# Causal attention with a row mask on TensorE: one mask product a head, log subtraction first, and the key-major exp ahead of the last row exp

## Chip, cores and metric

The kernel runs on one core of a Trainium2 chip. The time is device microseconds (us) from the first to the last instruction of one execution, and what frames it; the median of several executions is compared. A profile is one execution, recorded instruction by instruction.

## The reference

The input x is 16 sequences of 512 tokens, 128 wide. It is layer-normalised, and goes into two branches that are added to x.

```python
xn  = layernorm(x)
q, k, v = xn @ Wq, xn @ Wk, xn @ Wv           # 16 heads, q and k 8 wide, v 64 wide
scores  = einsum('bhqd,bhkd->bhqk', q, k) / sqrt(8)
scores  = where(key > query, -inf, scores)     # causal
ctx = einsum('bhqk,bhkd->bhqd', softmax(scores), v)
xr, xk = mu * xn + (1 - mu) * shifted(xn)      # one mu each
ffn = sigmoid(xr @ W_r.T) * (relu(xk @ W_k.T)**2 @ W_v.T)
out = x + ctx @ Wo + ffn
```

## The kernel before

**Two passes over the scores.** The scores of a head are made twice. In the row-major pass (queries on partitions) the kernel makes masked scores, takes each row's maximum on VectorE (DVE), and lets ScalarE (ACT) take exp of them, in place in PSUM, only for the sum of each row. Ln of the sums and the maximum make one number a row, which is appended to q as two more rows of the contraction. In the key-major pass, ten units of work later, the scores come out of TensorE (PE) transposed and already normalised, and one exp gives the attention weights; GpSimd (POOL) zeroes the triangle above the diagonal, and PE weighs v with them.

**Units.** Work is cut into units, five to a group, where a group is two head pairs (four heads), and a batch (one sequence) has four groups, so 20 units a batch and 320 in all. The five kinds of a unit, 0 to 4, are rows of the tables `ROWS` (row-major blocks, lines 301 to 307) and `KEYS` (key-major blocks, lines 309 to 315). Each unit fills a PSUM tile `sm` of 128x1024 (row-major, two buffers) and a PSUM tile `sT` of 128x1024 (key-major, one buffer). Kinds 0 and 2 of the row pass have four row exps (two 384 wide, two 128 wide), kinds 1 and 3 have two (512 wide), kind 4 has four (256 wide). Every row exp is an ACTIVATE and a read of its accumulator.

**Order.** No scheduler moves anything: every engine's instructions run in the order in which `unit_work` (line 531) issues them, held there by the `_InOrder` wrappers (line 32, whose call is the L42 of most profile rows). In unit n the key-major pass works on unit n, the row exps on unit n + 10, and the row scores, mask and row maximum on unit n + 11. So a row exp in unit n uses the maximum from unit n - 1, and the row scores of unit n need the `sm` buffer that the row exps of unit n - 1 gave back.

In unit n PE does: `rowscores`, `scores`, `rowmask`, the listed pieces (in kind 1 after `weigh`), `weigh`, and in kind 0 `turn_stats`. DVE does: `take_ctx` (kinds 0 and 2), `rowmax`, the pieces, and in kind 0 `sub_logs` as the last piece and then `turn_stats`. ACT does: all row exps (`rowsum`), in kind 4 the Ln (`log_sums`), then the key-major exp (`weights`).

**Pieces.** The table `todo` (line 490) spreads the next sequences' projections over the units: `project_v`, `project_qk` (the q part in unit 10, the k part in unit 15 of a batch, each followed by two DVE conversions `qh, ql` or `kh, kl`), the feed-forward steps, `project_out` and so on. Pieces that need a PSUM tile take it from `m_tile` (line 150). From unit -1 on, all of them, the `pm` tile of `turn_stats` too, share one buffer; before that three are used in turn.

**The mask.** `rowmask` (line 341) adds a large negative number above the diagonal of each 128x128 diagonal block by a product of a 64-row bf16 identity (`id64`) with 64 rows of a bf16 mask (`mask64`). It takes two products a head, one for each half of the queries (`c`), the first 128 columns wide for each block and the second 64; with two heads that is four products a unit.

Of the kernel before, what the change touches and what calls it, by code (L numbers as in the profile page):

```python
# [9 lines left out]
FP = mybir.dt.float32  # L10
FR = mybir.dt.float32r
BF = mybir.dt.bfloat16
AF = mybir.ActivationFunctionType
ALU = mybir.AluOpType
# [3 lines left out]
P = 128  # L18
# [6 lines left out]
UNITS = 5  # L25
LEAD = 10
EPS = 1e-5
MASKED = -3.0e38
SIG_MIN = -87.5


# [16 lines left out]
def attn_ffn_kernel(  # L48
# [32 lines left out]
    const = ctx.enter_context(tc.tile_pool(name="const", bufs=1))  # L81
# [3 lines left out]
    one = ctx.enter_context(tc.tile_pool(name="one", bufs=1))  # L85
# [11 lines left out]
    pe, dve, act = _InOrder(tc, nc.tensor), _InOrder(tc, nc.vector), _InOrder(tc, nc.scalar)  # L97
    pool, sp = _InOrder(tc, nc.gpsimd), _InOrder(tc, nc.sync)
# [10 lines left out]
    for name, w in (("wq", Wq), ("wk", Wk)):  # L109
        t = one.tile([P, H * DK], FP, tag=f"{name}_n", name=f"{name}_n")  # L110
# [5 lines left out]
    for i, w in enumerate((W_r, W_k, W_v)):  # L116
        t = one.tile([P, D], FP, tag=f"ffn_n{i}", name=f"ffn_n{i}")
# [10 lines left out]
    ident = const.tile([P, P], FP, tag="ident", name="ident")  # L128
# [3 lines left out]
    fill = const.tile([3, 2, T], FP, tag="fill", name="fill")  # L132
# [157 lines left out]
    def ffn_out(b):  # L290
# [10 lines left out]
    ROWS = (  # L301
        ((0, 2, 0), (0, 0, 384)),
        ((0, 3, 0),),
        ((1, 2, 0), (1, 0, 384)),
        ((1, 3, 0),),
        ((0, 1, 0), (1, 1, 256)),
    )
# [11 lines left out]
    def unit_of(n):  # L319

        n, t = divmod(n, UNITS)
        b, g = divmod(n, NPAIR // 2)
        return (b, g, t) if 0 <= b < B else None


    stats, sms = {}, {}
# [14 lines left out]
    def rowmask(b, g, t):  # L341

        ends = [to + (i + 1) * P for _, i, to in ROWS[t]]
        step = ends[-1] - ends[0] or P
        for c in range(2):
            for u in range(2):
                s = slice(64 * u, 64 * u + 64)
                cols = sms[b, g, t][:, u, ends[0] - P :]
                if len(ends) > 1 and step > P:
                    cols = cols.rearrange("q (m k) -> q m k", k=P)[:, 0 :: step // P, 64 * c :]  # L350
                else:
                    cols = cols.rearrange("q (m k) -> q m k", k=P)[:, :, 64 * c :]
                pe.matmul(
                    cols, id64[s, c, :],
                    mask64[s, c : c + 1, 64 * c :].to_broadcast([64, len(ends), P - 64 * c]),
                    start=False, stop=(c == 1),
                )

    def rowmax(b, g, t):
        if t == 0:  # L360
# [14 lines left out]
                negm[:, :, w, i], sm[:, :, to : to + (i + 1) * P], AX.X, ALU.max, negate=True  # L375
            )

    def rowsum(b, g, t):
        negm, z = stats[b, g]
        sm = sms.pop((b, g, t))  # L380
        for w, i, to in ROWS[t]:
            for u in range(2):
                cols = sm[:, u, to : to + (i + 1) * P]
                act.activation(
                    cols, cols, AF.Exp,
                    bias=negm[:, u, w, i : i + 1], accum_out=z[:, u, w, i : i + 1],
                )

    def log_sums(b, g):
        lz = stat.tile([P, 2, 2, NB], FP, tag="lz", name=f"lz_{b}_{g}")  # L390
# [3 lines left out]
    def sub_logs(b, g):  # L394
        negm, z, lz = stats[b, g]
        dve.tensor_tensor(lz, negm, lz, ALU.subtract)
# [12 lines left out]
    def put_stats(b, g):  # L409

        for n, half in enumerate(stats.pop((b, g))):
            for u in range(2):
                r = 64 * u + RS + n
                pool.dma_start(
                    out=qs[b % 2].bitcast(FP)[r : r + 1, 2 * g : 2 * g + 2, :].rearrange(
                        "o p (i t) -> o (p i) t", t=P
                    ),
                    in_=half.bitcast(FP)[2 * NB * u : 2 * NB * u + 2 * NB],
                )
# [15 lines left out]
    def weights(b, g, t):  # L435
        e = ep.tile([P, 2, 512], FP, tag="e", name=f"e_{b}_{g}_{t}")
        act.activation(e, sts.pop((b, g, t)), AF.Exp)
        for w, j, to in KEYS[t]:

            diag = e[:, :, to : to + P]  # L440
            pool.affine_select(
                out=diag, in_=diag, compare_op=ALU.is_ge, fill=0.0, base=0,
                pattern=[[0, 2], [1, P]], channel_multiplier=-1,
            )
            es[b, 2 * g + w, j] = e[:, :, to : to + T - j * P]
# [41 lines left out]

    todo, turns, puts = {}, {}, {}  # L490

    def at(n, f, *args):
        todo.setdefault(n, []).append((f, args))
# [4 lines left out]
    for b in range(B):  # L498
        n0 = b * per
        if b + 1 < B:  # L500
            r = 0 if b else 7
            at(n0 + r, ffn_r, b + 1)
            at(n0 + r + 1, ffn_exp, b + 1)
            for c, n in enumerate((3, 8, 13, 18) if b else (11, 13, 14, 18)):
                at(n0 + n, ffn_sig, b + 1, c)
            for m, n in enumerate((1 if b else 3, 5, 12, 13, 14, 16, 17, 18)):
                at(n0 + n, project_v, b + 1, m // 2, m % 2)
            at(n0 + 7, mix_prev, b + 1, 1)
            at(n0 + 9, mix, b + 1, 1)
            at(n0 + 11, ffn_k, b + 1)  # L510
            at(n0 + 19, ffn_out, b + 1)
            for m, n in enumerate((-1, -1, 0, 0, 4, 4, 5, 5) if b else (0, 0, 0, 0, 4, 4, 5, 5)):
                at(n0 + n, spread_qk, b + 1, *SPREAD[m], slice(0, NPAIR // 2))
            for m, n in enumerate((8, 9, 9, 10, 10, 14, 14, 15)):
                at(n0 + n, spread_qk, b + 1, *SPREAD[m], slice(NPAIR // 2, NPAIR))
        if b + 2 < B:
            at(n0 + 4, deviation, b + 2)
            for c in range(NB):
                at(n0 + (1, 1, 3, 3)[c], row_moments, b + 2, c)
                at(n0 + 4 + c // 2, normalise, b + 2, c)  # L520
            at(n0 + 6, transpose_xn, b + 2)
            at(n0 + 10, project_qk, b + 2, False)
            at(n0 + 15, project_qk, b + 2, True)
            at(n0 + 12, mix_prev, b + 2, 0)
            at(n0 + 14, mix, b + 2, 0)
        for p, n in enumerate((2, 3, 3, 4, 7, 8, 8, 9) if b < B - 1 else (-8, -7, -7, -6, -3, -2, 0, 3)):
            at(n0 + per + n, project_out, b, p)
        if b + 3 < B:
            at(n0 + 11, load_x, b + 3)

    def unit_work(n):
        now, stat_now, stat_next = (unit_of(n + m) for m in (0, LEAD, LEAD + 1))
        if n in puts:
            put_stats(*puts.pop(n))

        if stat_next:
            rowscores(*stat_next)
        if now:
            scores(*now)
        if stat_next:  # L540
            rowmask(*stat_next)
        t = n % UNITS
        done = {0: (n - UNITS, 0), 2: (n - UNITS, 1)}.get(t)
        if done and unit_of(done[0]):
            b, g, _ = unit_of(done[0])
            take_ctx(b, 2 * g + done[1])
        if stat_next:
            rowmax(*stat_next)

        if stat_now:  # L550
            rowsum(*stat_now)
            b, g, kind = stat_now
            if kind == UNITS - 1:
                log_sums(b, g)
                at(n + 1, sub_logs, b, g)
                turns[n + 1] = puts[n + 2] = b, g
        if now:
            weights(*now)
        pieces = todo.pop(n, ())
        if t != 1:  # L560
            for f, args in pieces:
                f(*args)
        since, w, blocks = WEIGHED[t]
        if unit_of(n - since):
            b, g, _ = unit_of(n - since)
            for j in blocks:
                weigh(b, 2 * g + w, j, (t, j) in ((1, 3), (4, 3)))
        if t == 1:
            for f, args in pieces:
                f(*args)  # L570
        if n in turns:
            turn_stats(*turns.pop(n))
# [23 lines left out]
    for c in range(NB):  # L596
# [4 lines left out]

    tri = one.tile([P, P], FP, tag="tri", name="tri")
    pool.memset(tri, 0.0)
    pool.affine_select(
        out=tri, in_=tri, compare_op=ALU.is_ge, fill=MASKED, base=0,
        pattern=[[-1, P]], channel_multiplier=1,
    )
    id64 = const.tile([P, 2, P], BF, tag="id64", name="id64")  # L610
    mask64 = const.tile([P, 2, P], BF, tag="mask64", name="mask64")
    pool.memset(id64, 0.0)
    pool.memset(mask64, MASKED)
    for u in range(2):
        half = slice(64 * u, 64 * u + 64)
        for c in range(2):
            cols = slice(64 * c, 64 * c + 64)
            dve.tensor_copy(id64[half, c, cols], ident[half, half])
            dve.tensor_copy(mask64[half, c, cols], tri[half, half])

    make_qk(1)
    for pairs in (slice(0, 2), slice(2, 4)):
# [76 lines left out]
```

## Time and profile before

| what | value |
|---|---|
| median of 3 runs (range) | 1032.33 us (1031.92 to 1036.72) |
| the profiled execution, its time and its span | 1032.25 us, 1030.5 us |
| busy: PE, DVE, ACT, POOL | 961.6, 792.8, 923.9, 520.3 us |
| granted TensorE clock, mean of the span | 0.979 |
| row exps, ACTIVATE, 1024 of them | 513.1 us, mean 501 ns |
| key-major exps, 320 | 324.3 us, mean 1013 ns |
| mask products, 1280 | 103.0 us busy, mean 236 ns |
| row maxima, 448 | 398.9 us, mean 915 ns |

Busy time counts an instruction from start to end. PE's products overlap, and their mean duration is longer than the distance from one start to the next; where the text speaks of a product's cost it is that distance. In the timeline each row is: start in us from the span's start, us that the row covers, engine, line, operation, output and inputs with their forms, how many instructions were joined, and in brackets how long the engine had been idle before it and what ended that. A row "PEld" is a load of stationary weights, and "ACTIVATION_READ_ACCUMULATOR" is the second half of a row exp.

### The profile page before, as it was taken

To read this page: it belongs to the slowest core of one execution; us is meant where nothing else is said; L and a number is where in the kernel's file an instruction comes from. 1 tells how busy PE (TensorE), PEld (TensorE's weight loads), DVE (VectorE), ACT (ScalarE), POOL (GpSimd) and SP (SyncE) were. 2 spreads that over 40 slices of the span, in tenths; PEclk is the share of its full clock that TensorE was granted. 3 is DMA by queue.
4 is the path that set the end of the run, shared out by engine and by line. 5 is a ranking of instruction groups with operands and counts; after the bars stand their busy time and mean duration, and the time that the engine had idled before them with its cause. 6 is when DMAs were issued, how large, how long until landed. Compare 5 with 4: busy or idle time off the path is not lost.

```text
span 1030.5 us, 24120 instructions
## 1 busy us (share of the span) xinstructions
PE 961.6 (93%) x8771; PEld 525.6 (51%) x8771; DVE 792.8 (77%) x1316; ACT 923.9 (90%) x2449; POOL 520.3 (50%) x957
## 2 busy tenths in 40 slices
PE   3888999999999999999999999999999999999997
PEld 1334454545546464554645555464555646455454
DVE  4877878787787878788788877878878787877741
ACT  0788999999999999999999999999999999999982
POOL 4156454644646464464655546464464546444432
PEclk8679999999999999999999999999999999999999
DMA  7811515225250532625053252504425140433000
GB/s 193 147 23 44 104 25 104 32 67 90 54 104 10 108 42 53 105 54 99 8 109 49 54 105 53 94 14 100 57 54 95 34 97 4 98 49 49 3 13 11
DMA packets 59973, 67.19 MB, mean 65 GB/s; under 512 B 12928, under 2 KB 33024, under 8 KB 59856
## 3 DMA queue, kind: packets, MB, share of 16 engines
q1 hardware_dynamic: 48688, 61.89, 32.1%
q0 software_dynamic: 8640, 1.34, 1.0%
q10 hardware_dynamic: 2528, 2.43, 0.8%
q8 instruction: 70, 1.15, 0.5%
q14 instruction: 47, 0.39, 0.2%
HBM read 39.13 MB, written 25.17 MB: 62 GB/s over the span
## 4 chain that ended last, share of the span: by engine, by line
PE 57%; ACT 19%; DVE 17%; issue 6%; POOL 1%; DMA 0%; ACTq 0%; DVEq 0%; POOLq 0%
PE av L42 16%; ACT sm L42 13%; PE sm L42 12%; PE po L42 10%; DVE negm L42 7%; PE sT L42 7%; ACT e L42 6%; PE pv L42 6%; DVE sig L42 2%; PE pr L42 1%; DVE v L42 1%; PE pm L42 1%; PE pkv L42 1%; DVE xmix L42 1%; PE xnTp L42 1%
## 5 line engine op out<-in xcount | busy, mean ns | idle before, releaser
L42 ACT ACTIVATE sm<-sm,negm 128x384 f32<-128x384 f32 (+3 forms) x1024 | 513.1, 501 | 71.9 <-DMA q<-qh 25.4
L42 DVE TENSOR_REDUCE negm<-sm 128x2 f32<-128x768 f32 (+3 forms) x448 | 398.9, 915 | 125.4 <-PE sm L42 125.1
L42 POOL TENSOR_SCALAR_AFFINE_SELECT e<-e 128x256 f32<-128x256 f32 x512 | 208.2, 426 | 418.2 <-ACT e L42 416.0
L42 ACT ACTIVATE e<-sT 128x1024 f32<-128x1024 f32 x320 | 324.3, 1013 | 21.7 <-PE sT L42 21.7
L42 PE MATMUL av<-e,v 128*64 128x512 f32 (+3 forms) x2048 | 336.2, 439 | 1.3 <-POOL e L42 0.7
L42 PEld LDWEIGHTS av<-e,v 128*64 128x64 f32 x2048 | 138.1, 137 | 166.5 <-issue 139.2
L42 ACT ACTIVATION_READ_ACCUMULATOR sm<-sm,negm 128x1 f32 x1024 | 201.1, 196 | 0.0
L42 PE MATMUL sm<-k,q 33*128 33x384 f32 (+3 forms) x1024 | 163.7, 377 | 4.3 <-ACT sm L42 4.3
L42 PEld LDWEIGHTS sm<-k,q 33*128 33x128 f32 x1024 | 82.9, 188 | 149.0 <-ACT sm L42 72.7
L42 PE MATMUL sT<-q,k 35*128 35x512 f32 (+3 forms) x1024 | 146.5, 338 | 4.5 <-ACT e L42 4.3
L42 PE MATMUL pv<-wv,xnT 128*64 128x512 f32 x512 | 141.5, 632 | 6.9 <-DVE v L42 5.3
L42 PE MATMUL po<-wo,ctx 128*64 128x128 f32 x2048 | 133.2, 277 | 2.1 <-DVE ctx L42 1.6
L42 PEld LDWEIGHTS po<-wo,ctx 128*64 128x64 f32 x2048 | 109.8, 137 | 17.1 <-issue 9.7
L42 PEld LDWEIGHTS sT<-q,k 35*128 35x128 f32 x1024 | 90.2, 187 | 28.6 <-ACT e L42 22.6
L42 PE MATMUL sm<-mask,id 64*128 64x128 bf16 (+2 forms) x1280 | 103.0, 236 | 0.0
L42 DVE COPY v<-pv 128x512 f32<-128x512 f32 x128 | 85.9, 671 | 19.0 <-PE pv L42 18.9
L42 DVE COPY ctx<-av 128x512 f32<-128x512 f32 x128 | 87.3, 682 | 15.6 <-PE av L42 15.5
L42 POOL DMA_DIRECT2D q<-mh x128 | 69.8, 548 | 48.7 <-DVE mh L42 40.7
L42 POOL DMA_DIRECT2D q<-ml x128 | 65.9, 519 | 0.3 <-issue 0.3
L42 DVE RECIPROCAL sig<-e_sig 128x128 f32<-128x128 f32 x64 | 60.2, 941 | 0.0
L42 POOL TENSOR_SCALAR prev<-xnT,omm 128x512 f32<-128x512 f32 x32 | 50.0, 1563 | 12.8 <-DVE xmix L42 12.8
L42 PEld LDWEIGHTS <-id 64*128 64x128 bf16 x1280 | 40.1, 97 | 29.6 <-issue 15.7
(65 smaller groups left out, 568.4 us busy)
## 6 DMA issues: line engine op xcount, KB each, us to landing
q<-q SPq DMA_DIRECT2D x124, 128.0 KB, 4.9
k<-k SPq DMA_DIRECT2D x124, 128.0 KB, 5.5
k<-kh SPq DMA_DIRECT2D x30, 256.0 KB, 2.6
x<-in_L_attn_x_dram SPq DMA_DIRECT2D x16, 256.0 KB, 3.2
q<-qh SPq DMA_DIRECT2D x16, 256.0 KB, 4.2
q<-ql SPq DMA_DIRECT2D x16, 256.0 KB, 4.1
out_dram<-o SPq DMA_DIRECT2D x16, 256.0 KB, 2.8
k<-kl SPq DMA_DIRECT2D x15, 256.0 KB, 2.0
```

The costliest lines, as they stand in the source:

```text
L42: return self._tc.keep_in_program_order(f(*args, **kwargs))
```

## The change

There are three parts, and a few small ones that come with them.

1. **The mask as one product a head.** The two 64-row halves are replaced by a 64x128 matrix `id2`, in which each of the 64 rows serves two queries, with the weights 1 and 2^-84, and a 64x128 mask `mask2` whose entries are 0, -2^43 and -2^127. A unit has two mask products, each 128 columns wide for each diagonal block. Both matrices are cut from one `wide` tile, made on POOL with two memsets and four selects over 256 columns, and cast to bf16 by four DVE copies instead of eight.
2. **Logs first.** `sub_logs` of a group is no longer the last piece of kind 0 but comes right after `rowmask`, ahead of `take_ctx` and `rowmax` on DVE.
3. **The key-major exp before the last row exp.** `rowsum` calls `weights` before its last row exp, so that ACT's order in a unit is: all row exps but one, the key-major exp, the last row exp, and in kind 4 the Ln.

Also, `project_v` is now listed ahead of `ffn_sig`, so in units that have both, DVE copies v out of PSUM before it takes the reciprocal.

```diff
 def rowmask(b, g, t):
-        for c in range(2):
-            for u in range(2):
-                s = slice(64 * u, 64 * u + 64)
...
-                pe.matmul(
-                    cols, id64[s, c, :],
-                    mask64[s, c : c + 1, 64 * c :].to_broadcast([64, len(ends), P - 64 * c]),
-                    start=False, stop=(c == 1),
-                )
+        for u in range(2):
+            s = slice(64 * u, 64 * u + 64)
+            cols = sms[b, g, t][:, u, ends[0] - P :].rearrange("q (m k) -> q m k", k=P)
+            if len(ends) > 1:
+                cols = cols[:, 0 :: step // P, :]
+            pe.matmul(
+                cols, id2[s], mask2[s, None, :].to_broadcast([64, len(ends), P]),
+                start=False, stop=True,
+            )
...
-    def rowsum(b, g, t):
+    def rowsum(between, b, g, t):
         negm, z = stats[b, g]
         sm = sms.pop((b, g, t))
...
+        blocks = [(u, *block) for block in ROWS[t] for u in range(2)]
+        for m, (u, w, i, to) in enumerate(blocks):
+            if m == len(blocks) - 1:
+                between()
+            cols = sm[:, u, to : to + (i + 1) * P]
+            act.activation(
...
+            for m, n in enumerate((1 if b else 3, 5, 12, 13, 14, 16, 17, 18)):
+                at(n0 + n, project_v, b + 1, m // 2, m % 2)
             for c, n in enumerate((3, 8, 13, 18) if b else (11, 13, 14, 18)):
                 at(n0 + n, ffn_sig, b + 1, c)
-            for m, n in enumerate((1 if b else 3, 5, 12, 13, 14, 16, 17, 18)):
-                at(n0 + n, project_v, b + 1, m // 2, m % 2)
...
         if stat_next:
             rowmask(*stat_next)
+        if n in subs:
+            sub_logs(*subs.pop(n))
...
-        if stat_now:
-            rowsum(*stat_now)
+        attend = (lambda: weights(*now)) if now else lambda: None
+        if not stat_now:
+            attend()
+        else:
+            rowsum(attend, *stat_now)
             b, g, kind = stat_now
             if kind == UNITS - 1:
                 log_sums(b, g)
-                at(n + 1, sub_logs, b, g)
-                turns[n + 1] = puts[n + 2] = b, g
-        if now:
-            weights(*now)
+                subs[n + 1] = turns[n + 1] = puts[n + 2] = b, g
...
+    wide = one.tile([P, 2, 2 * P], FP, tag="wide", name="wide")
+    pool.memset(wide[:, 0, :], 0.0)
+    pool.memset(wide[:, 1, :], -FAR / NEAR)
+    for i, keep, base, value in (
+        (0, ALU.not_equal, 0, 1.0), (0, ALU.not_equal, -1, NEAR),
+        (1, ALU.is_ge, -2, -FAR), (1, ALU.is_ge, -1, 0.0),
+    ):
+        pool.affine_select(
...
+    for u in range(2):
+        half = slice(64 * u, 64 * u + 64)
+        for i, to in enumerate((id2, mask2)):
+            dve.tensor_copy(to[half], wide[half, i, P * u : P * u + P])
```

More of the change, by code (lines that the diff above doesn't have):

```diff
@@ L27 @@
 EPS = 1e-5
-MASKED = -3.0e38
+FAR, NEAR = 2.0**43, 2.0**-84
 SIG_MIN = -87.5
@@ L344, in rowmask @@
         step = ends[-1] - ends[0] or P
-        for c in range(2):
-            for u in range(2):
-                s = slice(64 * u, 64 * u + 64)
[L348 to L352, printed above, removed]
-                pe.matmul(
-                    cols, id64[s, c, :],
-                    mask64[s, c : c + 1, 64 * c :].to_broadcast([64, len(ends), P - 64 * c]),
-                    start=False, stop=(c == 1),
-                )
+        for u in range(2):
[7 more added lines that the diff above has]
+            )
     def rowmax(b, g, t):
@@ L376, in rowmax @@
             )
-    def rowsum(b, g, t):
+    def rowsum(between, b, g, t):
         negm, z = stats[b, g]
         sm = sms.pop((b, g, t))
[L381 to L387, printed above, removed]
+        blocks = [(u, *block) for block in ROWS[t] for u in range(2)]
[4 more added lines that the diff above has]
+            act.activation(
+                cols, cols, AF.Exp,
+                bias=negm[:, u, w, i : i + 1], accum_out=z[:, u, w, i : i + 1],
+            )
     def log_sums(b, g):
@@ L484, in project_out @@
             sp.dma_start(out=out[b].rearrange("(c p) d -> p c d", p=P), in_=o)
-    todo, turns, puts = {}, {}, {}
+    todo, subs, turns, puts = {}, {}, {}, {}
     def at(n, f, *args):
@@ L600, in attn_ffn_kernel @@
     project_qk(0, True, act)
[L604 to L613, printed above, removed]
+    wide = one.tile([P, 2, 2 * P], FP, tag="wide", name="wide")
[6 more added lines that the diff above has]
+        pool.affine_select(
+            out=wide[:, i, :], in_=wide[:, i, :], compare_op=keep, fill=value, base=base,
+            pattern=[[1, 2 * P]], channel_multiplier=-2,
+        )
+    id2 = const.tile([P, P], BF, tag="id2", name="id2")
+    mask2 = const.tile([P, P], BF, tag="mask2", name="mask2")
     for u in range(2):
         half = slice(64 * u, 64 * u + 64)
[L616 to L619, printed above, removed]
+        for i, to in enumerate((id2, mask2)):
+            dve.tensor_copy(to[half], wide[half, i, P * u : P * u + P])
     make_qk(1)
```

## The prediction

> **What bounds the kernel now.** I read the page first, then the chain of waits, then the timeline of one group, then the distances between the 64 Ln instructions on ACT, since each group has just one.
>
> ```profile
> PE 961.6 (93%) x8771; PEld 525.6 (51%) x8771; DVE 792.8 (77%) x1316; ACT 923.9 (90%) x2449; POOL 520.3 (50%) x957
> ...
> PE 57%; ACT 19%; DVE 17%; issue 6%; POOL 1%; DMA 0%; ACTq 0%; DVEq 0%; POOLq 0%
> ```
>
> By the page PE is the bound (93%, 57% of the chain). The end of the timeline says otherwise: the last sequence has no next one to prepare, PE has little to do, and still a group takes 14.51 us from Ln to Ln:
>
> ```profile
> 983.46 0.22 ACT L42 ACTIVATE lz<-z 128x16 f32<-128x16 f32 x1
> ...
> 997.97 0.22 ACT L42 ACTIVATE lz<-z 128x16 f32<-128x16 f32 x1
> ```
>
> That is ACT alone, with every exp starting as its predecessor lets it go. From about 107 us to 925 us the four groups of a batch take 15.71, 15.20, 15.03 and 14.80 us, batch after batch: 60.73. ACT's own need is 4 x 14.51, and 0.51 for the one `e_sig` exp: 58.55. So ACT waits about 2.2 us a batch, and no saving on PE can give more than that, some 31 us over 14 batches. Where the waits are, the first group of the four (units 10 to 14 of a batch, 15.71 us) shows:
>
> ```profile
> 394.40 0.26 PE L42 MATMUL sm<-mask,id 64*128 64x128 bf16 x4
> ...
> 394.58 1.08 PE L42 MATMUL pq<-xnT,wq 128*64 128x512 f32 x4
> ...
> 396.95 0.69 DVE L42 TENSOR_TENSOR ql<-pq,qh 128x512 fp32r<-128x512 f32 x1
> ...
> 397.56 0.17 DVE L42 TENSOR_TENSOR lz<-negm,lz 128x16 f32<-128x16 f32 x1
> ...
> 397.87 0.27 PE L42 MATMUL pm<-ident,lz 128*16 128x128 f32 x1 [0.92 <-DVE lz L42]
> ...
> 398.07 0.50 PE L42 MATMUL sm<-k,q 33*128 33x384 f32 x4
> ...
> 398.41 0.45 PE L42 MATMUL sT<-q,k 35*128 35x256 f32 x4
> ...
> 398.70 0.34 PE L42 MATMUL sm<-mask,id 64*128 64x256 bf16 x4
> ...
> 398.96 1.02 ACT L42 ACTIVATE e<-sT 128x1024 f32<-128x1024 f32 x1 [0.48 <-PE sT L42]
> ...
> 400.47 0.56 ACT L42 ACTIVATE sm<-sm,negm 128x384 f32<-128x384 f32 x1 [0.48 <-DVE negm L42]
> ```
>
> PE stands 0.92 us before `pm`; the row scores, scores and mask behind it are late; ACT waits 0.48 for scores and 0.48 for the row maximum. The next group has 0.48 of it again (at 415.68), the last 0.20 (at 445.52).
>
> **Mask.** Start to next start: 0.18 us for four products in kind 0 (394.40 to 394.58), 0.27 in kinds 1, 3 and 4 (398.70 to 398.97). Two products cannot cost less than half (0.09, 0.135 saved), since the half that stays is the wider one; above, the whole saving could be lost (0). The Trainium skill's page "TensorE: Matmul & The Clock Gate", section "Wait — 56ns, not 53.3ns?", names a floor of some 62 ns that each MATMUL can cost in the sequencer. By it each unit would save 2 x 62 ns, 40 us of PE time over 320 units. But the row of kind 0 has 45 ns a product, below that floor, so here width counts as well; I take 0.075 and 0.105, which is 2 x 0.075 + 3 x 0.105 = 0.465 a group, 30 us of PE in all. It is off the path wherever PE waits for ACT or DVE anyhow; next to nothing of it arrives in the units discussed below.
>
> **Logs first.** The waits list has "PE pm <- DVE lz" at 24.5 us, but `pm` shares one PSUM buffer with `pq`, whose last reader `ql` ended at 397.64, 0.09 before `lz` (397.73). So in this group, and likewise in the one with `kl`, the conversion holds `pm`, and moving `lz` wins 0.09 and costs its own 0.10 ahead of `ctx`, `negm`, `qh` and `ql` on DVE: nothing. `lz` may also now wait for the Ln, with `take_ctx` and `rowmax` queued behind; kind 0 has 3.3 us on ACT to cover it. It wins only at the start, where the buffer is free: 0.97 us (43.66) and 1.49 us (57.05), of which I count 2.5.
>
> **The exp ahead of the last row exp.** This is the step that decides. The row scores of unit n+1 need the buffer of unit n's last row exp:
>
> ```profile
> 29.37 0.34 ACT L42 ACTIVATE sm<-sm,negm 128x128 f32<-128x128 f32 x1
> ...
> 29.63 0.19 ACT L42 ACTIVATION_READ_ACCUMULATOR sm<-sm,negm 128x1 f32 x1
> ...
> 29.73 0.65 ACT L42 ACTIVATE sm<-sm,negm 128x512 f32<-128x512 f32 x1
> ...
> 29.88 0.50 PE L42 MATMUL sm<-k,q 33*128 33x384 f32 x4 [1.47 <-ACT sm L42]
> ```
>
> PE starts 0.06 after the accumulator read (29.82), 0.17 after the exp. Before, PE could do row scores during the key-major exp, and that exp came again only after all row exps of the next unit (1.49 us and more). Afterwards, from the end of a last row exp: PE needs 0.17, row scores 0.34 (398.07 to 398.41), scores 0.45 (kind 1; 0.39 in kind 3, from 403.92), 0.10 to ACT (398.86 to 398.96): 1.06 and 1.00. ACT meanwhile has, in kinds 1 and 3, one row exp: 0.15 to its start, 0.67 to the exp (404.44 to 405.11), 0.83 rounded up. It loses 0.23 and 0.17, 0.40 a group, even where PE is on time. Kinds 0, 2, 4 have three row exps there (1.8 and more) and lose nothing. Against it, Ln now stands between row exps: it cost 0.26 (RA to exp 0.35 at 408.18, against 0.09 at 402.63), and by the nearest row (an exp starts 0.11 before the exp ahead of it ends) 0.12: 0.14 won, within 0 and 0.2. ACT's need becomes 14.37 a group.
>
> Where PE is late, kind 1 loses more, having so little cover. First group: the kind 3 unit ahead of it on PE is 3.42 (448.36 to 451.78, two output projections), 3.32 with the new mask, 0.76 behind ACT's release (0.83 + 0.90 + 0.66 + 0.17 = 2.56). Call the start of the kind 4 unit's row scores R. DVE takes the maximum 0.90 after R, is then busy to the end of `ql` without a pause for 5.60 (452.79 to 458.39), and 0.10 for `lz` in front; 0.34 to the row scores of kind 1, 0.89 to its exp (398.07 to 398.96): R + 7.83. ACT from the same R: exp of kind 4 at R + 0.89; last row exp ends 1.35 later, 2.24; 0.27 past Ln and 1.76 to the exp of kind 0, 4.27; 1.24 to its last row exp's end, 5.51; 0.83: R + 6.34. It loses 1.5. The second group, with `kh, kl` and no lateness ahead, gives by the same path R + 7.90 against R + 7.08: 0.8. The third (3.37 on PE in kind 0 against 3.27 on ACT) loses 0.3, the fourth about 0.3. So a batch is 4 x 14.37 + 0.51 + (1.5 + 0.8 + 0.3 + 0.3) + 4 x 0.17 = 61.6 us, 0.9 more than 60.73. The gain that it has is that the row maximum's wait (2 x 0.48) hides behind the last row exp; that is in the 61.6.
>
> **Small parts.** V copied before the reciprocal takes away two waits of 0.36 a batch in PE's kind 4 (as at 407.22): covered, as PE then waits for ACT's release; uncovered it would be 0.7 x 14 = 10 us. POOL's setup goes from 1.3 (0.21, 0.29, 0.38, 0.39) to about 2.5 (two memsets of 0.39, four selects of 0.43, from the rows of that width), so its four fill DMAs start at 10 instead of 8.84 and its next work is at 18.48: hidden; the casts wait for it only at 15.34. Four casts instead of eight, 0.10 apart: 0.4 earlier on the path to the first scores.
>
> **The sum.** 14 x 0.9 = 12.6; five last groups at 14.77 instead of 14.51: 1.3; start: -2.5 for the logs, -0.4 for the casts, -1.5 for masks at half clock (0.31 to 0.47 each there, half of the saving on the path), -1.3 for waits on the maximum in batch 0 (0.71 at 60.45, 0.58 at 67.19) that go behind the last row exp: -5.7. Together +8.2: a span of 1038.7, and with the 1.75 around it 1040.4; the page's execution is 0.1 below the median. As the late kinds were added at their full size I round down: **1039 us**, own range 1032 to 1046.
>
> **Rivals.** (1) Faster: the hand-back is no longer than its cover, 0.83 instead of 1.00 to 1.06. Then each kind 1 and 3 loses 0.2 less, 1.6 a batch: 60.0, 0.7 below before, so -10, -5.7 at the start: 1016. For it: the chain of waits has PE at 57%, PE loses 30 us of work, and the waits on the maximum end. Against it: the rows at 29.63 and 398.07. It decides as soon as the path is under 0.9. (2) Nothing net: logs and masks hidden, exp order neutral, because the losses in kind 1 replace the old ones one for one: 1033. (3) Larger loss: after standing idle PE's first products are slower, as scores are after a wait (mask 0.34 behind them at 409.59, 0.25 at 394.15). Then 0.10 more in eight places a batch, 12 us: 1051.
>
> **How the numbers follow.** Half a per cent, 5 us, is about what a measurement of this kernel tells from no change. The forecast has 0.50, of which 0.12 lies below 1037.5; rival 1 (1006 to 1026) 0.25; rival 2 (1027 to 1037) 0.13, of which 0.02 is faster; rival 3 0.12. Faster 0.27, same 0.23, slower 0.50. The range 1012 to 1050 leaves out the low end of rival 1 and the upper half of rival 3.
>
> **What would show it.** Ln to Ln near 15.9, 15.4, 15.3, 15.0 in a batch and 14.75 at the end; a wait "ACT e <- PE sT" that grows from 22 us to over 40 in kinds 1 and 3; a wait "ACT sm <- DVE negm" near zero after the start; PE idle before row scores, ended by ACT; `pm` waiting as long as now. The prediction is wrong if row scores start before the last row exp is over, if masks save over 0.2 a unit, or if Ln to Ln falls under 14.5.

## The result: 1.3 us slower, within half a per cent

| | before | after |
|---|---|---|
| median (range), 20 runs each | 1032.82 us (1031.1 to 1036.84) | 1034.11 us (1031.91 to 1037.63) |
| ratio, 95% interval | | 1.0017 (1.0007 to 1.0028) |
| span of the profiled execution | 1030.5 us | 1031.1 us |
| groups of a full batch, Ln to Ln | 15.71, 15.20, 15.03, 14.80 = 60.73 us | 15.75, 15.40, 14.99, 14.80 = 60.95 us |
| last groups | 14.51 us | 14.47 us |
| eighth Ln / last Ln | 149.77 / 997.97 us | 148.16 / 999.00 us |

The forecast was 1039 us and slower by over 0.5%. The time lies inside its range of 1032 to 1046, but the change is 5 us smaller than forecast, and less than the half per cent that the forecast called no change. The two lines of the page that opened the prediction now read:

```profile
PE 931.8 (90%) x8131; PEld 511.9 (50%) x8131; DVE 791.7 (77%) x1312; ACT 897.2 (87%) x2449; POOL 519.3 (50%) x959
...
PE 35%; ACT 35%; DVE 18%; issue 8%; DMA 2%; POOL 1%; SPq 0%; ACTq 0%; POOLq 0%
```

PE lost 30 us of busy time, half of it in the mask rows (103.0 to 87.5), and its share of the chain fell from 57% to 35%, yet the time did not fall. ACT, now 35% of the chain (19% before), lost 27 us of busy time although it runs the same 2449 instructions: more of its accumulator reads now lie under the start of the next exp. That is a first trace of what the forecast had missed. The Ln rows of the last groups, 14.47 apart where 14.77 was forecast, and just under the 14.5 that the forecast had named as a sign that it is wrong:

```profile
984.53 0.21 ACT L44 ACTIVATE lz<-z 128x16 f32<-128x16 f32 x1
...
999.00 0.22 ACT L44 ACTIVATE lz<-z 128x16 f32<-128x16 f32 x1
```

The waits lists (engine, tile, who released it: us in all, times, longest), of the kernel before and of the changed one:

```profile
PE pm L42 <- DVE lz L42: 24.5, 31, 2.0
...
ACT e L42 <- PE sT L42: 21.7, 28, 1.9
ACT sm L42 <- DVE negm L42: 20.0, 37, 1.7
...
PE sm L42 <- ACT sm L42: 4.3, 5, 1.5
```

```profile
ACT e L44 <- PE sT L44: 77.1, 135, 2.5
...
PE sm L44 <- ACT sm L44: 35.5, 90, 1.7
...
PE pm L44 <- DVE ql L44: 12.8, 14, 0.9
...
PE pm L44 <- DVE kl L44: 12.6, 14, 0.9
...
ACT sm L44 <- DVE negm L44: 4.1, 5, 1.4
```

Four of the forecast's marks stand. The key-major exp's wait for scores went from 21.7 us (28 times) to 77.1 (135 times); 56 us of that lie before the exps of kind 1 and 15 before those of kind 3, each of which waits. The row exps' wait for the maximum went from 20.0 to 4.1. PE's wait for the `sm` buffer went from 4.3 to 35.5. And `pm` waits as long as before: 24.5 us then, 12.8 + 12.6 now, under the names of the conversions and no longer under that of `lz`. The first group of the batch at 445 us shows all of it in one place:

```profile
456.51 0.69 DVE L44 TENSOR_TENSOR ql<-pq,qh 128x512 fp32r<-128x512 f32 x1
...
457.35 0.27 PE L44 MATMUL pm<-ident,lz 128*16 128x128 f32 x1 [0.94 <-DVE ql L44]
...
458.45 1.02 ACT L44 ACTIVATE e<-sT 128x1024 f32<-128x1024 f32 x1 [1.55 <-PE sT L44]
```

The logs were ready at 454.2, three microseconds before `pm`; `pm` still starts after `ql`. ACT, which before lost 0.48 here for scores and 0.48 for the maximum, now loses 1.55 for scores alone (forecast: 1.5).

### The profile page after: what moved, and what is told of

It reads as the page before. It is cut to its first block, busy times and chain, and to the rows that moved or that the text cites. A ratio compares the mean times of both kernels' runs of the same rounds, so it can differ in the third digit from the quotient of the medians.

```text
span 1031.1 us, 22839 instructions
## 1 busy us (share of the span) xinstructions
PE 931.8 (90%) x8131; PEld 511.9 (50%) x8131; DVE 791.7 (77%) x1312; ACT 897.2 (87%) x2449; POOL 519.3 (50%) x959
## 3 DMA queue, kind: packets, MB, share of 16 engines
q8 instruction: 65, 1.06, 0.5%
## 4 chain that ended last, share of the span: by engine, by line
PE 35%; ACT 35%; DVE 18%; issue 8%; DMA 2%; POOL 1%; SPq 0%; ACTq 0%; POOLq 0%
ACT sm L44 19%; ACT e L44 15%; PE sm L44 10%; PE av L44 8%; PE po L44 7%; DVE negm L44 6%; PE sT L44 5%; DVE v L44 2%; DVE xmix L44 2%; PE pv L44 2%; PE pr L44 1%; PE pm L44 1%; DVE sig L44 1%; DVE kl L44 1%; DVE kh L44 1%
## 5 line engine op out<-in xcount | busy, mean ns | idle before, releaser
L44 POOL TENSOR_SCALAR_AFFINE_SELECT e<-e 128x256 f32<-128x256 f32 x512 | 206.1, 422 | 388.8 <-ACT e L44 388.7
L44 ACT ACTIVATE e<-sT 128x1024 f32<-128x1024 f32 x320 | 326.0, 1019 | 78.0 <-PE sT L44 77.1
L44 ACT ACTIVATION_READ_ACCUMULATOR sm<-sm,negm 128x1 f32 x1024 | 206.4, 202 | 0.0
L44 PE MATMUL sm<-k,q 33*128 33x384 f32 (+3 forms) x1024 | 164.6, 376 | 43.9 <-ACT sm L44 35.5
L44 PE MATMUL pv<-wv,xnT 128*64 128x512 f32 x512 | 139.1, 622 | 2.3 <-DVE ffn L44 0.4
L44 PE MATMUL sT<-q,k 35*128 35x512 f32 (+3 forms) x1024 | 138.2, 324 | 1.6 <-DMA q<-ml 1.3
L44 DVE COPY v<-pv 128x512 f32<-128x512 f32 x128 | 87.5, 684 | 17.7 <-PE pv L44 17.7
L44 DVE COPY ctx<-av 128x512 f32<-128x512 f32 x128 | 87.3, 682 | 12.7 <-PE av L44 12.6
L44 PE MATMUL sm<-mask,id 64*128 64x256 bf16 (+1 forms) x640 | 87.5, 263 | 0.0
L44 PEld LDWEIGHTS <-id 64*128 64x128 bf16 x640 | 33.3, 95 | 33.2 <-issue 25.0
```

What stands on the lines that cost most here:

```text
L44: return self._tc.keep_in_program_order(f(*args, **kwargs))
```

## What was not forecast: the hand-over from one unit to the next

ACT of the changed kernel from the last row exp of a kind 0 unit through the kind 1 unit to the first row exp of kind 2, and PE's row scores and scores in that stretch:

```profile
972.84 0.34 ACT L44 ACTIVATE sm<-sm,negm 128x128 f32<-128x128 f32 x1
973.09 0.21 ACT L44 ACTIVATION_READ_ACCUMULATOR sm<-sm,negm 128x1 f32 x1
973.18 0.67 ACT L44 ACTIVATE sm<-sm,negm 128x512 f32<-128x512 f32 x1
973.75 0.22 ACT L44 ACTIVATION_READ_ACCUMULATOR sm<-sm,negm 128x1 f32 x1
974.24 1.02 ACT L44 ACTIVATE e<-sT 128x1024 f32<-128x1024 f32 x1 [0.27 <-PE sT L44]
...
975.73 0.20 ACT L44 ACTIVATION_READ_ACCUMULATOR sm<-sm,negm 128x1 f32 x1
975.83 0.56 ACT L44 ACTIVATE sm<-sm,negm 128x384 f32<-128x384 f32 x1
```

```profile
973.35 0.50 PE L44 MATMUL sm<-k,q 33*128 33x384 f32 x4 [0.40 <-ACT sm L44]
973.69 0.45 PE L44 MATMUL sT<-q,k 35*128 35x256 f32 x4
```

The path by PE is the forecast one: the exp at 972.84 ends at 973.18, the row scores start 0.17 later, the key-major exp at 974.24, 1.06 after the row exp's end (forecast 1.06). But the row exp that covers it starts at 973.18, at once, where the forecast had "0.15 to its start". From the start of the accumulator read to the next row exp is 0.09 here (973.09 to 973.18) and 0.10 in the next unit (975.73 to 975.83). Inside a unit it is 0.22 to 0.25, as in the kernel before:

```profile
406.37 0.21 ACT L42 ACTIVATION_READ_ACCUMULATOR sm<-sm,negm 128x1 f32 x1
...
406.62 0.45 ACT L42 ACTIVATE sm<-sm,negm 128x256 f32<-128x256 f32 x1
```

Counted over the whole trace: before, all 704 row exps that follow a row exp of their own unit directly start 0.22 to 0.25 after that accumulator read. After, the 394 such starts that are left take 0.22 to 0.25 too, and of 241 direct steps from one unit's last row exp to the next unit's first, 232 take 0.09 or 0.10. (232 reads that overlap the next exp by 0.12 are 28 us: the busy time that ACT lost.) In both traces every row exp but the first of its unit waits on ScalarE's own semaphore, as it writes in place into the tile that the exp ahead of it wrote too; the first one of a unit, on another `sm` tile, waits only for other engines.

So the theory (T in the expectations below, against the prediction's own account, P): the new order does two things to ACT. It puts the key-major exp between the last two row exps of a unit, so that the dear hand-over of 0.23 between them is gone; and it brings the unit's last row exp next to the following unit's first, which is a cheap one of 0.09. The forecast had booked a dear one there. That is about 0.14 in each of five units of a group by this first reading; the third run corrected the number of places.

## The experiments

In the expectations the sums of four groups of a full batch are given beside the time. "Batch" is that sum from the profile of the run. The kernel before had medians of 1032.43, 1032.64 and 1032.01 us in the three series; each ratio is to the one on the same chip. A difference of two medians and the same difference by the ratios disagree by up to about 1 us here, so single microseconds prove little.

**1. The exp order alone.** The kernel before, with part 3 of the change only: old mask, logs last.

```diff
+        for m, (u, w, i, to) in enumerate(blocks):
+            if m == len(blocks) - 1:
+                between()
...
+        attend = (lambda: weights(*now)) if now else lambda: None
...
-            rowsum(*stat_now)
+            rowsum(attend, *stat_now)
...
-        if now:
-            weights(*now)
```

> The kernel before with part 3 alone (key-major exp ahead of the last row exp; masks and logs as before). Theory T, the hand-over: the last row exp of a unit and the first of the next one are 0.09 us apart from read to start (0.23 inside a unit), so each unit wins about 0.13 on ACT, which pays for waits on scores in kinds 1 and 3: last groups 14.5 us from Ln to Ln, batches about 61.3, time 1036 to 1041. Rival P, the prediction's own sum (no cheaper hand-over): last groups 14.77, batches about 62, time about 1048.

Measured: 1038.43 us (1037.96 to 1040.85), ratio 1.0062 (1.0049 to 1.0074); batch 61.18; last groups 14.45 to 14.52. The order alone costs 6.0 us, where P, by the same steps, had 1048 us and last groups of 14.77. The last groups show best that the loss was put too high: PE has little to do there, and ACT is no slower than before.

**2. Mask and logs without the exp order.**

```diff
-            if m == len(blocks) - 1:
-                between()
...
             if kind == UNITS - 1:
                 log_sums(b, g)
                 subs[n + 1] = turns[n + 1] = puts[n + 2] = b, g
+            attend()
```

> The changed kernel with the key-major exp put back behind all row exps. Theory T with the measured mask (0.03 and 0.06 us saved a unit, not 0.075 and 0.105): batches about 60.4, time 1024 to 1029. Rival P (masks save 0.465 a group, start saves 5.7): 1014 to 1020. Rival Q, the exp order is worth nothing net and logs and masks are hidden: as after, 1034.

Measured: 1026.6 us (1026.25 to 1029.09), ratio 0.995 (0.9937 to 0.9962); batch 60.38 (15.74, 15.03, 15.03, 14.57); last groups 14.51. So parts 1 and 2 win 5.8 us (5.2 by the ratio), and part 3 on top of them costs 7.5 (1026.6 to 1034.11; 6.9 by the ratios). The two nearly cancel. With part 3 in place parts 1 and 2 win only 4.3 (1038.43 to 1034.11).

**3. The forecast's hand-over put back.** All row exps write into one SBUF scratch tile. Sums are the same; the exp values, which nobody reads, go elsewhere. Now every row exp shares its output tile with the one before it, across units too.

```diff
+    scrp = ctx.enter_context(tc.tile_pool(name="scrp", bufs=1))
...
+            junk = scrp.tile([P, 512], FP, tag="junk", name=...)[:, 0 : (i + 1) * P]
             act.activation(
-                cols, cols, AF.Exp,
+                junk, cols, AF.Exp,
```

> The changed kernel, with all row exps writing to one and the same scratch tile in SBUF instead of in place, so that the first row exp of a unit has to wait for the last one of the unit before, as inside a unit; the sums it takes are the same. Theory T: the hand-over across units becomes 0.23, 5 x 0.13 a group come back, last groups 14.75 or more, batches about 61.6, time about 1043. Rival: the 0.09 has nothing to do with that wait, or the hand-over plays no part: as after, 14.47 and 1034.

Measured: 1045.81 us (1045.07 to 1047.1), ratio 1.0126 (1.0111 to 1.0142); batch 61.66; last groups 14.75. The forecast for the changed kernel had a batch of 61.6 and last groups of 14.77. The time is 3 us above the 1043 expected. Of the 635 direct hand-overs 627 are now 0.22 to 0.25, and the other eight are longer. Its ACT in a kind 1 unit:

```profile
986.60 0.37 ACT L44 ACTIVATE junk<-sm,negm 128x128 f32<-128x128 f32 x1
986.85 0.21 ACT L44 ACTIVATION_READ_ACCUMULATOR junk<-sm,negm 128x1 f32 x1
987.09 0.69 ACT L44 ACTIVATE junk<-sm,negm 128x512 f32<-128x512 f32 x1
...
988.00 1.02 ACT L44 ACTIVATE e<-sT 128x1024 f32<-128x1024 f32 x1
```

0.24 from read to exp (986.85 to 987.09) instead of 0.09. The key-major exp comes 1.40 after the start of the last row exp of the unit ahead (986.60 to 988.00), and in the changed kernel too (972.84 to 974.24): in kind 1 PE sets its start, and the cheaper hand-over becomes a longer wait for scores. The last groups tell where it counts. Start to start over one group (984.53 to 999.00 against 983.82 to 998.57) the two traces differ in six steps only: into the first row exp of kinds 1, 2, 3 and 4 the one with the scratch tile takes 0.15, 0.15, 0.15 and 0.13 more, and from there to the key-major exp of kinds 1 and 3 it takes 0.15 and 0.14 less. The fifth place has the Ln between, and is the same in both. So of five places four have the cheap hand-over, two of these hand it over to the wait for scores, and two keep it: 0.28 to 0.29 a group, 14.47 against 14.75.

**4. The hand-over made cheap in the kernel before.** Two scratch tiles in turn, nothing else.

```diff
+    scrp = ctx.enter_context(tc.tile_pool(name="scrp", bufs=2))
...
-                    cols, cols, AF.Exp,
+                    junk, cols, AF.Exp,
```

> The kernel before, with row exps writing in turn to two scratch tiles in SBUF instead of in place, so that no row exp has to wait for the one just ahead of it. Theory T: the hand-over inside a unit falls from 0.23 to 0.09 in eleven places a group; the last groups, where ACT alone sets the pace, go from 14.5 to about 13.1; full batches only to about 60.2, since PE and DVE are next; time about 1017. Rival: 0.23 is the price of reading the accumulator, whatever the output: 14.5, and 1032.

Measured: 1017.89 us (1014.2 to 1019.48), ratio 0.9853 (0.9834 to 0.9872); batch 60.05; last groups 13.27 to 13.65. With two tiles all 704 hand-overs inside a unit are 0.09 or 0.10:

```profile
963.93 0.19 ACT L42 ACTIVATION_READ_ACCUMULATOR junk<-sm,negm 128x1 f32 x1
964.02 0.57 ACT L42 ACTIVATE junk<-sm,negm 128x384 f32<-128x384 f32 x1
```

Runs 3 and 4 both write to SBUF and differ in whether consecutive exps share a tile. Output in SBUF is thus not what makes the hand-over cheap (an exp to SBUF is itself 0.02 to 0.03 longer); sharing the tile with the exp just ahead is what makes it dear. Run 9 below says so more cleanly: it differs from run 3 in having two scratch tiles for one, and nothing else, and takes 1013.58 us for 1045.81. Nor is it the wait on ScalarE's semaphore as such. In run 4, 640 of the 704 exps still carry that wait, but their tile was last written two exps before, and they start at 0.09. Eleven places a group at 0.14 are 1.5; the last groups win 0.9 to 1.2, the full batches 0.17 a group. There ACT now waits for others:

```profile
ACT e L42 <- PE sT L42: 57.4, 71, 2.3
ACT junk L42 <- DVE negm L42: 38.2, 91, 1.9
```

**5. Mask alone,** with v copied before the reciprocal.

It is the changed kernel with logs and exp order put back:

```diff
-            if m == len(blocks) - 1:
-                between()
...
-        if n in subs:
-            sub_logs(*subs.pop(n))
...
+            attend()
+        if n in subs:
+            pieces = [*pieces, (sub_logs, subs.pop(n))]
```

> The kernel before with the new mask and v copied before the reciprocal; logs stay last, exps in their old order. If the logs are worth nothing in full batches (the conversion holds the shared PSUM buffer): as with the logs first, batches about 60.4, time 1026 to 1029. If the 24.5 us that the list of waits puts on the logs were theirs: nearly all of the gain of masks and logs is gone, 1031 to 1033.

Measured: 1029.65 us (1027.06 to 1032.69, 22 runs), ratio 0.9968 (0.9958 to 0.9978); batch 60.41. That lies between the two bands expected, 0.65 us above the first. The mask and the order of v together win 3.0 us; they were not told apart.

**6. Logs last again in the changed kernel.**

```diff
-        if n in subs:
-            sub_logs(*subs.pop(n))
...
+        if n in subs:
+            pieces = [*pieces, (sub_logs, subs.pop(n))]
```

> The changed kernel with the log subtraction put back as the last piece of kind 0. Logs worth nothing in full batches: within 2 us of the changed kernel, 1032 to 1036, batches about 60.95, the wait before the turned logs as long. Logs worth what the list of waits says: slower by 10 us or more, over 1043.

Measured: 1037.15 us (1035.04 to 1040.51, 14 runs), ratio 1.004 (1.0027 to 1.0054); batch 60.91, against 60.95 with the logs first. About 1 us above the expected band, so the logs are worth 3.0 us by the medians (1037.15 to 1034.11; 2.4 by the ratios), and the same again without the exp order (1029.65 to 1026.6; 1.9 by the ratios). In both pairs the full batches are equal within 0.04. The gain is thus outside them: from the first to the eighth Ln logs last take 110.13 us and logs first 108.11, and without the exp order 111.27 and 109.83. Those are 2.0 and 1.4 us at the start, where the forecast had 2.5.

**7. The exp order only where its cover is long** (kinds 0, 2 and 4; in kinds 1 and 3 the key-major exp stays behind all row exps).

```diff
-            if m == len(blocks) - 1:
+            if m == len(blocks) - 1 and len(blocks) > 2:
                 between()
...
+            if len(ROWS[kind]) < 2:
+                attend()
```

> The changed kernel with the key-major exp ahead of the last row exp only in kinds 0, 2 and 4; in kinds 1 and 3, which have two row exps, it comes behind both. Theory T: three of the five cheap hand-overs stay (3 x 0.13 a group) and the waits on scores in kinds 1 and 3 go, batches about 60.2, time 1020 to 1026, below both the changed kernel and the one with the old order. Rival: kind 1 and 3 are not where the loss is (PE's or DVE's work alone sets the batches): no better than the changed kernel, 1032 to 1036.

Measured: 1021.28 us (1019.54 to 1022.34), ratio 0.9881 (0.9859 to 0.9903); batch 60.08; last groups 14.21 to 14.34. So the loss of part 3 is in kinds 1 and 3, as the forecast said, and the rest of part 3 is a gain: 5.3 us better than no reordering (1026.6), 12.8 better than reordering everywhere. ACT's wait for scores falls to 30.0 us (39 times).

**8 and 9. Cheap hand-overs with the old exp order and with the new.** Both have the new mask, logs first and two scratch tiles as in run 4; run 8 has the key-major exp behind the row exps, run 9 ahead of the last.

> New mask, logs first, exps in their old order, row exps writing in turn to two scratch tiles. Theory T: no row exp waits for the one ahead, and PE has the shorter mask: batches about 59.1, last groups below 13.5, time about 1004. Rival: PE with DVE sets full batches once ACT is free of its waits, and the mask's saving does not reach it: about 60.0 a batch, 1015 to 1018 as with the scratch tiles alone.

Measured (run 8): 1005.69 us (1004.83 to 1008.17), ratio 0.9737 (0.9714 to 0.9759); batch 59.18 (15.63, 15.11, 14.23, 14.21).

> The changed kernel, all three parts, with row exps writing in turn to two scratch tiles. Here no hand-over is dear, so the new exp order can win none, and only its waits on scores in kinds 1 and 3 are left. Theory T: slower than the same kernel with the old exp order (1005.7) by 8 to 14 us, 1014 to 1020, batches about 60.0. Rival, the exp order helps by hiding waits on the row maximum: 1000 to 1006.

Measured (run 9): 1013.58 us (1009.79 to 1014.51), ratio 0.9812 (0.9788 to 0.9836); batch 59.57. Once hand-overs are cheap anyway, part 3 has nothing to win by them and costs 7.9 us (just under the 8 to 14 expected). The wait for scores, 47.5 us in run 8, is 93.0 in run 9; that for the maximum, 36.2 in run 8, is 6.3:

```profile
ACT e L44 <- PE sT L44: 93.0, 116, 3.2
...
ACT junk L44 <- DVE negm L44: 6.3, 8, 1.9
```

**10. The fastest version.** Run 8's first group of a batch stayed at 15.63. There the `mix` piece (SCALAR_TENSOR_TENSOR, 0.82) stands on DVE right ahead of `lz`, `ctx`, `negm`, `qh` and `ql`, and so ahead of `pm`. It was moved one unit forward.

```diff
-            at(n0 + 9, mix, b + 1, 1)
+            at(n0 + 8, mix, b + 1, 1)
```

> As the kernel with scratch tiles, new mask, logs first and the old exp order, with the mixing of the feed-forward input moved one unit earlier (from unit 9 to unit 8 of a batch), out of the DVE work that holds the turned logs in unit 10. If DVE's chain up to the conversion sets that group: its 15.6 us fall by up to 0.6, time 997 to 1003; if PE or POOL sets it: 1005 as before.

Measured: 994.92 us (992.25 to 999.14), ratio 0.9649 (0.9614 to 0.9683); batch 58.59; the first group 15.04. That beats both kernels, by 37 and 39 us, and lies 2 us under the expected band: besides the full batches, the eighth Ln comes 4.5 us earlier than in run 8 (142.68 for 147.19). PE's wait before `pm` in that group, in run 8 and then in run 10:

```profile
448.87 0.27 PE L44 MATMUL pm<-ident,lz 128*16 128x128 f32 x1 [0.94 <-DVE ql L44]
```

```profile
440.86 0.27 PE L44 MATMUL pm<-ident,lz 128*16 128x128 f32 x1 [0.44 <-DVE ql L44]
```

It is 0.50 shorter, and the group 0.59. In the second group, where another `mix` piece stands right ahead of the logs (459.76 and 451.73) and was not moved, the wait stays at 0.94 and the group at 15.13 (15.11). What moving that one would bring was not tried.

## Why the prediction was wrong, step by step

**The failed step: the cover of the path in kinds 1 and 3.** The term "0.15 to its start", added to 0.67 for the row exp, took the hand-over inside a unit for that between units. It is 0.09 after the read, about nothing after the exp's end. The fence under that step already had it: the read at 29.63 and the exp of the next unit at 29.73 are 0.10 apart, while the text used rows inside units for ACT's need. By itself a shorter cover makes the loss in kinds 1 and 3 larger, by 0.14 each; but the same 0.14 also goes out of ACT's need in kinds 1 to 4, and that was never booked. Corrected, ACT's need is 14.37 - 4 x 0.14 = 13.81, the loss in kinds 1 and 3 is 0.40 + 2 x 0.14 = 0.68, and a last group 14.49 instead of 14.77; measured 14.47. In full batches 4 x 0.28 = 1.1 would come off 61.6; 0.65 did (60.95). The rest lies mainly in two terms that were too small: ACT's idle time ahead of the exp of kind 1 is 1.55, 1.21, 0.27 and 0.58 in the four groups, where 1.5, 0.8, 0.3 and 0.3 were forecast, and 0.16 in each kind 3, where it was 0.17. (The two can be compared: the shorter cover adds 0.14 to a forecast loss, and the idle time counts only from the end of the accumulator read, 0.12 after the earliest start.) Run 3, 11.7 us slower than the changed kernel, gives the forecast's batch and last group back when the forecast's hand-over is put in, and run 4 moves the same hand-over in the kernel before. Run 3 does not give back the forecast's time: it takes 1045.81 us, not 1039, as its eighth Ln comes at 152.31, 2.5 later than before, where the forecast had the start 5.7 earlier. A start forecast too favourably thus hid part of the error in the batches; that the time fell inside the range is partly luck.

**The sum, with what each term did.** The forecast had +8.2 us from start to last Ln, and +1.0 was measured. Full batches: 14 x (0.22 - 0.9) = -9.5. Last groups: 5 x (-0.04 - 0.26) = -1.5. Start: -1.6 instead of -5.7, +4.1. Together -6.9, of the -7.2 to be explained.

**Right:** the path from a last row exp to the key-major exp (1.06 forecast and measured in kind 1; in kind 3, 993.31 to 994.25, 0.94 against 1.00); the place of the loss (run 7); the first group's lateness (1.55 against 1.5); the vanishing wait for the maximum; the logs, worth nothing in full batches because `pm` waits for the buffer that `ql` and `kl` read last, and about 2 at the start where 2.5 were forecast (run 6).

**Mis-sized: the mask.** Its saving was taken as 0.075 and 0.105 a unit, 0.465 a group. From start to next start in the changed kernel the two products take 0.16 to 0.17 (128 columns, before 0.18 to 0.20) and 0.21 (256 columns, before 0.27):

```profile
976.57 0.23 PE L44 MATMUL sm<-mask,id 64*128 64x128 bf16 x2
...
976.73 0.54 PE L44 MATMUL po<-wo,ctx 128*64 128x128 f32 x5
```

That is 0.02 to 0.03 and 0.06, some 0.22 a group, half of what was taken. Over 64 groups it is 14 us of PE; the time saw 3.0, together with the order of v (run 5). Next to nothing was to arrive in full batches; with the order of v, 0.32 a batch did (60.73 to 60.41). Halving the number of products saved between a tenth and a seventh of the time in the narrow form and a fifth in the wide one. The floor of some 62 ns a MATMUL, which the Trainium skill's page "TensorE: Matmul & The Clock Gate", section "Wait — 56ns, not 53.3ns?", gives for decoding without the hardware decoder, would have made it 0.124 in both. No run here shows which decoding was in use; at 45 ns a product before the change, that floor did not bind. The measurement was below that price and below the forecast's, and between the forecast's ends (0, and 0.09 and 0.135).

**Mis-sized: the start.** The -1.5 for masks at half clock and the -1.3 for waits on the maximum did not show as such. From the first to the eighth Ln the changed kernel wins 2.4 us (110.54 to 108.11), and 2.0 of these go away with logs last (run 6), so some 0.4 is left for both. The first Ln itself comes 0.8 later (39.23 and 40.05). One profile each can't explain that: over the twelve kernels it lies anywhere from 39.2 to 42.6 us. It stays open.

**The rivals.** Rival 2 (nothing net) named the right time, 1033, for a wrong reason: logs and mask are not hidden (5.8 us, run 2), and the exp order is not neutral (+6.0, run 1). Two effects of the same size cancel. Rival 1 needed a hand-back path under 0.9; it was 1.06 and 0.94. Rival 3's extra 0.10 on products after a pause is not in the rows above: after 0.40 of idleness row scores and scores take 0.34 and 0.29 from start to start (973.35, 973.69, and the mask at 973.98), as at 398.07 before. Nor is it in kind 3 of the changed kernel, where scores take 0.24 at the median behind row scores that PE began after more than 0.3 of idleness (31 times). Before, they took 0.33 there with no idleness ahead (55 times).

## What to carry to other kernels

When instructions of one engine are reordered, look at the gap between each pair that becomes neighbours, in rows that have just that pair, and at what each waits for; the same two operations can stand 0.23 or 0.09 us apart, depending on whether they share an output tile. An exp that is wanted only for its accumulated sum should not write where the previous one wrote: two scratch tiles in turn were worth 15 us of 1032 here, where the mask and the logs together won 5.8. And before an instruction is moved forward on one engine, compare the path by the other engine with the cover that remains, kind by kind; where the cover was long the move won 5 us, where it was short it lost 13.

## What the runs showed of the hardware

- An exp with an accumulator that follows another one starts 0.09 to 0.10 us after the start of the accumulator read when the two write different tiles, and 0.22 to 0.25 when they write the same tile, so that the second waits, by ScalarE's own semaphore, for the first (704 places in the kernel before, all dear; the same 704 in run 4, all cheap).
- A wait on that semaphore costs nothing when the exp waited for is not the one just ahead: the last row exp of a unit, which has the same wait, starts 0.90 after the start of a 128x1024 key-major exp of 1.01 (986.41 to 987.31 in the changed kernel), as the first row exp of a unit does before, without that wait (395.99 to 396.89).
- An exp of PSUM into SBUF took 0.02 to 0.03 longer than one in place in PSUM (means of run 3 and of the changed kernel, 128x384: 0.578 against 0.551; 128x128: 0.368 against 0.342).
- Two mask products of 128 columns take 0.16 to 0.17 us from start to next start, where four of 128 and 64 columns took 0.18 to 0.20.
